# Two-layer graph attention in fp32: mask as a PSUM seed for half of the score banks, and reciprocals on ScalarE and GpSimd

## The chip, the cores and the metric

The kernel runs on one core of a Trainium2 chip. The metric is the device time of one execution in microseconds (us); the median of three runs is used. All data are fp32.

## The reference, cut to what matters

Two layers act on x of shape (64, 256, 512), 64 batches of 256 nodes with 512 features, with one adjacency matrix `adj` (256 x 256) shared by all batches.

```python
h = relu(layernorm(x))
x = x + (adj @ h) @ W0 + b0                       # layer 0
h = relu(layernorm(x))
q, k, v = h @ Wq + bq, h @ Wk + bk, h @ Wv + bv   # layer 1, 8 heads of 64
s = q @ k.T / 8 + (1 - adj) * -1e9                # per batch and head
x = x + softmax(s) @ v @ Wo + bo
```

`adj` holds fractions, so the mask (1 - adj) * -1e9 is large nearly everywhere. The softmax needs the row's largest mask subtracted before the exponential; the kernel calls that row vector `top`.

## The kernel before, in words

**Tiling.** The batches are taken in 32 groups of two (`GB = 2`, `NG = 32`). Layer 0 runs over all groups, from 20 to some 640 us, and leaves each group's residual and its normalized, transposed hidden rows in DRAM. Layer 1 then runs over all groups. A matrix product by a weight is done by `project` (seven quarter products in place of eight) and, from group 2 on (`FIRST2`), by `project2`, which takes three of the seven apart once more, with PSUM banks for inner sums.

**Layer 0.** For each group the generator `layer0(g)` (tiles w_g) is interleaved with `adjacency(g + 1)` (tiles py_g+1). Both use three banks called a, c and b. Banks a and c of w are seeded: ScalarE copies the bias b0 into them, and the matmuls add to it.

**Layer 1, one half of the heads (`qd`) at a time.** The loop is: `attend(g, 0)`, `score(g, 1)`, queries and keys of group g + 1, `attend(g, 1)`, `score(g + 1, 0)`, values of g + 1, then `post(g)`, the output projection.

- `score` works through four pairs of banks, (c, b) = 00, 01, 10, 11. For each pair TensorE writes transposed scores (L974), then VectorE reads both banks with `scalar_tensor_tensor` (L980): scores times 1/8 plus the mask `maskT`, into the tile `a` in SBUF. GpSimd subtracts `top` (L986), except in a few stages where VectorE does it (L984). ScalarE takes the exponential (L991), GpSimd adds the two key halves (L998).
- `attend` forms the denominators `pden` (L1007) and the products with v, `pav` in two banks (L1014). ScalarE copies pden to `den` and sums it (L1023). VectorE inverts it in four pieces (L1027), two at once and two later from group 2 on. `divide` multiplies both pav banks by the inverse (L1045), and `note` sums the inverse on ScalarE (L1039). The sums are checked against a bound at the end (L1174, L1175); where they exceed it, a general path, not taken here, would compute everything again.

**What sets the order.** The program order on each engine is that of the Python code: instructions are queued as the functions are called. `after(n, fn)` puts work off by n ticks of a clock that advances between products. Each engine runs its queue in order, and waits are put in where data require them. DMAs are issued on SyncE, but for the first few on ScalarE.

**PSUM banks.** There are eight, handed out by `bank` (L248) from the list `free_banks` and returned to its end by `give` (L258). A list `whole` keeps, for each bank, whether its last tenant's matmuls wrote all of it. [...] a seeded request needs a bank that is whole. `project2` gives its inner banks back as not whole. Before, an unseeded request takes the first bank in the list:

```python
i = next(i for i in free_banks if seed is None or whole[i])
```

A new tenant's first write to a bank must wait until the last reading of the old tenant has ended.

Of the kernel before, what the change touches and what calls it, by code (L numbers as in the profile page):

```python
# [10 lines left out]
AF = mybir.ActivationFunctionType  # L11
ALU = mybir.AluOpType
AX = mybir.AxisListType
P = 128
EPS = 1e-5
SCALE = 1.0 / 8.0
MASKED = -1000000000.0

BOUND = 1.0e22


def load_weight(nc, pool, w, name):
# [176 lines left out]
def kernel(  # L199
# [16 lines left out]
    nc = tc.nc  # L216
    B, N, D = x.shape
    H, HD = 8, D // 8
    DC = D // P
    NT = N // P  # L220
    GB = 2
    T = GB * NT
    GN = GB * N
    NG = B // GB
    HQ = 2
    HF = D // 2
    assert (N, D, HD, GN) == (256, 512, 64, 512)

    keep = ctx.enter_context(tc.tile_pool(name="keep", bufs=1))
    stats = keep.tile([P, 2, NG * HQ], F32, name="stats")  # L230
    flag = keep.tile([1, 1], I32, name="flag")
# [13 lines left out]

    free_banks, bank_of, whole = list(range(8)), {}, [False] * 8

    def bank(shape, name, seed=None):  # L248

        i = next(i for i in free_banks if seed is None or whole[i])  # L250
        free_banks.remove(i)
        t = psum.tile(shape, F32, tag=f"bank{i}", name=name)
        bank_of[id(t)] = (i, t)
        if seed is not None:
            nc.scalar.copy(t, seed[:, None, :].to_broadcast(shape))
        return t

    def give(t, all_written=True):  # L258
        i = bank_of.pop(id(t))[0]
        free_banks.append(i)  # L260
        whole[i] = all_written
# [16 lines left out]
    X, H0, Q, K, V, OT = {}, {}, {}, {}, {}, {}  # L278
# [229 lines left out]
    FIRST2 = 2  # L508
# [32 lines left out]
    def project2(n, halves, blocks, by_token, name, place, first, done=None, seeds=(), add_up=False):  # L541
# [3 lines left out]
        s = W[n]  # L545
# [66 lines left out]
        yield  # L612
        inner = []
        for a, i, k, own in (("a12", 0, 0, None), ("a22", 1, 0, pc), ("s4", 0, 1, pa)):
            inner.append(Inner(a, i, k, own, bank([P, 2, P], f"{name}{i}{k}")))
            inner[-1].u1()
        p2, p4, p3 = inner
        for p in inner:
            if p is not p3 or add_up:
                p.add(p.sum, 0, 0)  # L620
            else:
                p3.begin(p3.sum, 0, 0)
        p2.own = pb = bank([P, 2, N], f"{name}b")
        p2.only((0, 0), (0, 1), (1, 0), fresh=True)

        for m, n in ((0, N), (1, P)) if add_up else ((slice(0, 3), P),):
            o, u = (t if add_up else t.rearrange("p m (h j) -> p (m h) j", j=P) for t in (p2.o, pb))
# [44 lines left out]
        nc.vector.tensor_tensor(row[:, HF:], row[:, HF:], row[:, :HF], op=ALU.subtract)  # L672

    def seeded(row, name):
        return tuple(bank([P, 2, N], f"{name}{b}", seed=row[:, h * HF:(h + 1) * HF]) for h, b in enumerate("ac"))


    def ready(g, moments_at, scales_at, relus_at, batches=1):
# [280 lines left out]
        else:  # L959
            yield from project2("o", halves, O2.pop(g), True, f"o_{g}", place, add_to, done, seeds, add_up=True)  # L960

    A, AS = {}, {}

    def score(g, qd, sum_delay, exps=(3, 4, 5, 8)):


        pair = [act.tile([P, GB, 2 * NT, N], F32, tag="h", name=f"a_{g}_{qd}_{c}", bufs=2) for c in range(2)]
        for c in range(2):
            for b in range(GB):
                ps = [bank([P, NT * N], f"sc_{g}_{qd}_{c}{b}_{j}") for j in range(2)]  # L970
                q, k = Q[g][qd, b], K[g][qd, b]
                for kt in range(NT):
                    for j in range(2):
                        nc.tensor.matmul(ps[j][:, kt * N:(kt + 1) * N],  # L974
                                         k[j * HD:(j + 1) * HD, c, kt * P:(kt + 1) * P],
                                         q[j * HD:(j + 1) * HD, c, :], start=(kt == 0), stop=True,
                                         skip_group_check=True)
                a = A[c, b] = pair[c][:, b]
                for j in range(2):
                    nc.vector.scalar_tensor_tensor(a[:, j * NT:(j + 1) * NT, :].rearrange("p k n -> p (k n)"),  # L980
                                                   ps[j], SCALE, maskT_f, op0=ALU.mult, op1=ALU.add)
                    give(ps[j])
                if (g == NG - 1 or (g, qd) == (0, 0)) and c + b == 2:
                    after(2, lambda a: nc.vector.tensor_tensor(a, a, top_b, op=ALU.subtract), a)  # L984
                else:
                    nc.gpsimd.tensor_tensor(a, a, top_b, op=ALU.subtract)  # L986
                after(exps[2 * c + b], exponent, a)
                after(sum_delay + 2 * c + b, key_sum, g, qd, c, b)

# [10 lines left out]
    def attend(g, qd):  # L1000


        pd = bank([P, GN], f"pden_{g}_{qd}")
        po = [bank([P, GN], f"pav_{g}_{qd}_{f}") for f in range(2)]
        for b in range(GB):
            for h in range(4):
                nc.tensor.matmul(pd[h * 32:(h + 1) * 32, b * N:(b + 1) * N], ones[:, 0:32], AS[h // 2, b][:, h % 2, :],  # L1007
                                 start=(b == 0), stop=True, tile_position=(0, h * 32), skip_group_check=True)
        for b in range(GB):
            v = V[g][qd, b]  # L1010
            for k in range(NT):
                for f in range(2):
                    for h in range(4):
                        nc.tensor.matmul(po[f][h * 32:(h + 1) * 32, b * N:(b + 1) * N],  # L1014
                                         v[:, k, h * HD + f * 32:h * HD + f * 32 + 32],
                                         A[h // 2, b][:, (h % 2) * NT + k, :],
                                         start=(b + k == 0), stop=(k == NT - 1), tile_position=(0, h * 32),
                                         skip_group_check=True)
        i = g * HQ + qd
        if i == 0:  # L1020
            AS["rest"] = act.tile([P, 4, GN], F32, tag="yT1", name="rest")
        den, rden = AS["rest"][:, 0, :], AS["rest"][:, 1, :]
        nc.scalar.activation(den, pd, AF.Identity, accum_out=stats[:, 0, i:i + 1])  # L1023
        give(pd)

        def invert(c):
            nc.vector.reciprocal(rden[:, c * P:(c + 1) * P], den[:, c * P:(c + 1) * P])  # L1027

        early = 2 if g >= FIRST2 and (g, qd) != (NG - 1, 1) else 4
        for c in range(early):  # L1030
            invert(c)
        if qd == 0:

            last = g == NG - 1
            OT[g] = (xpool if last else act).tile([P, DC, GN], F32, tag="x" if last else "r", name=f"oT_{g}")
            HO[g] = Halves(f"o_{g}", [OT[g][:, :, k * N:(k + 1) * N] for k in range(GB)], 0 if last else 1)

        def note():
            nc.scalar.activation(den, rden, AF.Identity, accum_out=stats[:, 1, i:i + 1])  # L1039

        def divide():
            for c in range(early, 4):
                invert(c)
            for f in range(2):
                nc.vector.tensor_tensor(OT[g][:, 2 * qd + f, :], po[f], rden, op=ALU.mult)  # L1045
                give(po[f])
            after(2 if (g, qd) == (NG - 1, 1) else 3, note)
            wait = 0
            if qd == 0:
                HO[g].sums(nc.gpsimd, ("t1",))  # L1050
            elif g < NG - 2:
                HO[g].sums(nc.gpsimd, ("t3", "t2", "t4"))
            elif g == NG - 2:
                wait = 8
                after(7, HO[g].sums, nc.gpsimd, ("t3",))
                after(8, HO[g].sums, nc.vector, ("t2",))
                after(8, HO[g].sums, nc.gpsimd, ("t4",))
# [77 lines left out]
    run(values(0))  # L1135
    for g in range(NG):
        attend(g, 0)
        load_residual(g)
        if g + 2 < NG:
# [3 lines left out]
        if g == 0:  # L1143
            for n, tag in ((4 * DC, "w0_sb"), (4, "w0_s1"), (4, "w0_s2"), (4, "w0_s4"), (4, "adjT"), (4, "b0_r")):
                t = const.tile([P, n, P], F32, tag=tag, name=f"spare_{tag}")
# [6 lines left out]
        else:  # L1152
            last = post(g - 1, seed_outputs(g - 1))
            run(last, 6)
        attend(g, 1)
        if g + 1 < NG:
            score(g + 1, 0, 5)
# [13 lines left out]

    bad = tmp.tile([P, 2 * NG * HQ], F32, tag="u", name="bad")
    worst = small.tile([P, 1], F32, tag="worst", name="worst", bufs=1)
    nc.vector.tensor_scalar(bad, stats.rearrange("p s i -> p (s i)"), BOUND, None, op0=ALU.is_gt)  # L1174
    nc.vector.tensor_reduce(worst, bad, AX.X, ALU.max)  # L1175
    run(last, 3)
    pf = bank([1, 1], "pf")
    nc.tensor.matmul(pf, worst, ones[:, 0:1], start=True, stop=True)
# [37 lines left out]
```

## Time and profile before

| what | us |
|---|---|
| three timed runs | 2660.87, 2661.75, 2664.04 |
| median | 2661.75 |
| profiled execution, from its first to its last instruction | 2658.7 |

The profiled execution is given as its span alone; the median of the timed runs is 3.05 us above it, which is what lies around the instructions.

| engine | busy us | share |
|---|---|---|
| TensorE, matmuls | 2624.0 | 99% |
| TensorE, weight loads | 2282.2 | 86% |
| GpSimd | 1981.1 | 75% |
| VectorE | 1869.5 | 70% |
| ScalarE | 970.5 | 37% |

Operations that the change touches, with their count, mean duration and the engine:

| line, operation | engine | count | mean ns |
|---|---|---|---|
| L986, top subtracted | GpSimd | 253 | 2369 |
| L980, scores read with the mask | VectorE | 512 | 680 |
| L1027, reciprocal of 128 columns | VectorE | 256 | 919 |
| L1023, denominators to SBUF | ScalarE | 64 | 597 |
| L974, score matmuls (passes) | TensorE | 2048 | 383 |

In the views PE is TensorE's matmul row and PEld its weight loads, DVE is VectorE, ACT ScalarE, POOL GpSimd and SP SyncE. A row of the view in order of time gives the start, the time from the start of the first to the end of the last of several equal instructions, engine, line, operation, and tiles as out<-in with the number of instructions; in brackets stands how long the engine was idle before it and what ended that. A row of the waits gives who waited, for whom, how long in all, how many times, and the longest. An fp32 matmul appears as two passes.

### The profile page before, as it was taken

The numbers are of one execution on the slowest core, as the hardware profiler recorded it, in microseconds if no ns is written. First come the engines' busy times: TensorE is split into PE (matmuls) and PEld (weight loads), VectorE is DVE, ScalarE is ACT, GpSimd is POOL, SyncE is SP. The second block draws the span as 40 slices with busy tenths as digits, with TensorE's granted clock in tenths as the row PEclk, the third lists the DMA queues.
The fourth block names the chain that finished last, engine by engine and source line by source line (L and its number), as shares of the span: only waits on it lengthen the run. The fifth ranks groups of instructions, "written<-read, shape, count | busy, mean of one in ns | idle before, by whom it ended". The sixth has DMA issues, their size and how long they took to land. (4 is left out here: it accounts for less than half of the span.)

```text
span 2658.7 us, 51781 instructions
## 1 busy us (share of the span) xinstructions
PE 2624.0 (99%) x20076; PEld 2282.2 (86%) x20076; DVE 1869.5 (70%) x3864; ACT 970.5 (37%) x1875; POOL 1981.1 (75%) x1838
## 2 busy tenths in 40 slices
PE   7999999999999999999999999999999999999997
PEld 6999899998888888888888888888888888888886
DVE  5878888885467676667677676667677676666677
ACT  3445454443333333333333333333333333333332
POOL 5888888775788777777777777777777777777775
PEclk9999999999999999999999999999999999999999
DMA  5777666665122111111111111111222111111110
GB/s 132 199 193 187 172 166 175 175 158 127 34 60 51 49 49 48 49 49 49 49 48 49 49 49 49 49 48 51 62 66 62 50 49 48 49 49 49 49 48 34
DMA packets 281066, 211.04 MB, mean 79 GB/s; under 512 B 145904, under 2 KB 212976, under 8 KB 280816
## 3 DMA queue, kind: packets, MB, share of 16 engines
q1 hardware_dynamic: 280352, 207.15, 29.9%
q8 instruction: 161, 2.64, 0.4%
q14 instruction: 89, 0.73, 0.1%
q10 hardware_dynamic: 464, 0.52, 0.1%
HBM read 106.96 MB, written 100.66 MB: 78 GB/s over the span
## 5 line engine op out<-in xcount | busy, mean ns | idle before, releaser
L986 POOL TENSOR_TENSOR a<-a,top 128x1024 f32<-128x1024 f32 x253 | 591.2, 2369 | 478.0 <-DVE a L980 478.0
L980 DVE SCALAR_TENSOR_TENSOR a<-sc,maskT 128x512 f32<-128x512 f32 x512 | 311.8, 680 | 122.8 <-PE sc L974 122.8
L998 POOL TENSOR_TENSOR as<-a 128x512 f32<-128x512 f32 x256 | 318.5, 1276 | 3.0 <-ACT a L991 3.0
L991 ACT ACTIVATE a<-a 128x1024 f32<-128x1024 f32 x256 | 270.9, 1058 | 4.3 <-DVE a L984 2.3
L1027 DVE RECIPROCAL rest<-rest 128x128 f32<-128x128 f32 x256 | 224.3, 919 | 36.1 <-ACT rest L1023 36.1
L974 PE MATMUL sc<-q,k 64*128 64x256 f32 x2048 | 239.0, 383 | 0.0
L1014 PE MATMUL pav<-a,v 128*32 128x256 f32 x4096 | 233.6, 379 | 0.0
L974 PEld LDWEIGHTS sc<-q,k 64*128 64x128 f32 x2048 | 194.7, 187 | 44.9 <-issue 26.3
L1014 PEld LDWEIGHTS pav<-a,v 128*32 128x32 f32 x4096 | 133.4, 110 | 87.9
L1023 ACT ACTIVATE rest<-pden 128x512 f32<-128x512 f32 x64 | 38.2, 597 | 417.7 <-PE pden L1007 417.7
L665 DVE TENSOR_TENSOR k<-k,k 128x128 f32<-128x128 f32 (+1 forms) x300 | 96.0, 352 | 126.3 <-PE k L564 123.9
L42 DVE BATCH_NORM_STATS2 st<-x 128x6 f32<-128x512 f32 x256 | 173.1, 676 | 9.4 <-DMA x<-in_x_dram 7.2
L693 ACT ACTIVATE h<-x,nb,rs 128x512 f32<-128x512 f32 x128 | 93.9, 803 | 69.3 <-POOL nb L54 69.2
L820 ACT ACTIVATE h<-x,nb,rs 128x512 f32<-128x512 f32 x128 | 97.2, 808 | 52.2 <-POOL nb L54 49.0
L665 DVE TENSOR_TENSOR x<-o,x 128x128 f32<-128x128 f32 (+1 forms) x360 | 110.9, 349 | 3.4 <-PE o_24b L564 0.3
L665 DVE TENSOR_TENSOR q<-q,q 128x128 f32<-128x128 f32 (+1 forms) x300 | 96.0, 352 | 14.0 <-PE q L564 11.7
L665 DVE TENSOR_TENSOR v<-v,v 128x128 f32<-128x128 f32 (+1 forms) x300 | 95.3, 351 | 14.4 <-PE v L564 11.3
L754 POOL TENSOR_TENSOR hs<-h 128x512 f32<-128x512 f32 x31 | 39.4, 1270 | 73.8 <-ACT h L693 63.7
L446 POOL TENSOR_TENSOR t_o<-oT,t_o 128x512 f32<-128x512 f32 x62 | 79.2, 1277 | 12.3 <-DVE t_o L446 10.0
L446 POOL TENSOR_TENSOR t_y<-yT 128x512 f32<-128x512 f32 (+1 forms) x65 | 81.8, 1258 | 5.9 <-ACT yT L804 5.9
L446 POOL TENSOR_TENSOR t_h<-h1T,t_h 128x512 f32<-128x512 f32 x64 | 82.0, 1282 | 5.0
L52 POOL TENSOR_TENSOR rs<-rs,mhalf 128x2 f32<-128x2 f32 (+1 forms) x97 | 79.5, 820 | 8.1
(4808 smaller groups left out, 6981.8 us busy)
## 6 DMA issues: line engine op xcount, KB each, us to landing
x<-in_x_dram SPq DMA_DIRECT2D x256, 128.0 KB, 3.1
residual<-x SPq DMA_DIRECT2D x256, 128.0 KB, 2.5
hidden<-r SPq DMA_DIRECT2D x128, 256.0 KB, 4.4
h1T<-hidden SPq DMA_DIRECT2D x64, 512.0 KB, 9.7
x<-residual SPq DMA_DIRECT2D x32, 1024.0 KB, 7.7
out_dram<-x SPq DMA_DIRECT2D x62, 512.0 KB, 4.3
w_sb<-in_L_gnn_weight_dram SPq DMA_DIRECT2D x1, 1024.0 KB, 9.8
wq_sb<-in_L_gnn_Wq_dram SPq DMA_DIRECT2D x1, 1024.0 KB, 8.2
```

Source lines behind the costliest of these rows:

```text
L42: nc.vector.bn_stats(st, src)
L446: eng.tensor_tensor(self.t[n][:, c, :], self.operand(p, c), self.operand(q, c), op=ALU.subtract)
L665: nc.vector.tensor_tensor(o, ps, u, op=ALU.add)
L693: nc.scalar.activation(H0[g][:, t, :], xt[:, t, :], AF.Relu, bias=nb[:, t % n:t % n + 1], scale=rs[:, t % n:t % n + 1])
L820: nc.scalar.activation(h1[:, k * NT + t, :], xt[:, k * NT + t, :], AF.Relu, bias=nb[:, t:t + 1], scale=rs[:, t:t + 1])
L974: nc.tensor.matmul(ps[j][:, kt * N:(kt + 1) * N], k[j * HD:(j + 1) * HD, c, kt * P:(kt + 1) * P], q[j * HD:(j + 1) * HD, c, :], start=(kt ...
L980: nc.vector.scalar_tensor_tensor(a[:, j * NT:(j + 1) * NT, :].rearrange("p k n -> p (k n)"), ps[j], SCALE, maskT_f, op0=ALU.mult, op1=ALU.add)
L986: nc.gpsimd.tensor_tensor(a, a, top_b, op=ALU.subtract)
L991: nc.scalar.activation(a, a, AF.Exp)
L998: nc.gpsimd.tensor_tensor(AS[c, b], a4[:, :, 0, :], a4[:, :, 1, :], op=ALU.add)
L1014: nc.tensor.matmul(po[f][h * 32:(h + 1) * 32, b * N:(b + 1) * N], v[:, k, h * HD + f * 32:h * HD + f * 32 + 32], A[h // 2, b][:, (h % 2) * ...
L1027: nc.vector.reciprocal(rden[:, c * P:(c + 1) * P], den[:, c * P:(c + 1) * P])
```

## The change

- **Scores.** At the start of `score` four banks, for the pairs (0, 0) and (0, 1), are seeded by ScalarE with 8 times `maskT`. Their matmuls add to it, and VectorE's reading subtracts `top` in the same instruction. The pairs with c = 1 stay as they were, with the mask added where VectorE reads and `top` subtracted by GpSimd or VectorE.
- **Reciprocals.** But for the very last stage, `den` is inverted by ScalarE as exp(-ln(den)), and GpSimd improves the result by one Newton step of three instructions. The exponential also sums the inverse, so `note` is left to the last stage. These instructions are queued behind the next stage's four seeds (`behind_seeds`).
- **Banks.** `bank` gets an argument `partial`. A request takes the first free bank whose `whole` is true, or false with `partial=True`, and the first free one if there is none of the wanted sort. `project2`'s inner banks, pden and one of the two pav banks ask for `partial=True`; all other requests, in both layers, do not.
- **Order of the attention products.** The loop over the two pav banks is moved outside.
- **Seeds** are made with `mul` in place of `copy`. ScalarE's table set, one with logarithm and exponential, is loaded at the start of the program. The check at the end is turned round (largest of "too large" becomes one minus the smallest of "small enough", one instruction more) and has a lower bound.

```diff
+    nc.scalar.preload_act_table_set("natural_log_exp_and_others")
...
-    def bank(shape, name, seed=None):
-
-        i = next(i for i in free_banks if seed is None or whole[i])
+    def bank(shape, name, seed=None, times=1.0, partial=False):
+
+        i = next((i for i in free_banks if whole[i] != partial), None if seed is not None else free_banks[0])
...
-            nc.scalar.copy(t, seed[:, None, :].to_broadcast(shape))
+            nc.scalar.mul(t, seed, times)
...
-            inner.append(Inner(a, i, k, own, bank([P, 2, P], f"{name}{i}{k}")))
+            inner.append(Inner(a, i, k, own, bank([P, 2, P], f"{name}{i}{k}", partial=True)))
...
-        p2.own = pb = bank([P, 2, N], f"{name}b")
+        p2.own = pb = bank([P, 2, N], f"{name}b", partial=True)
...
+        def banks(c, b, **how):
+            return [bank([P, NT * N], f"sc_{g}_{qd}_{c}{b}_{j}", **how) for j in range(2)]
+
+        masked = {cb: banks(*cb, seed=maskT_f, times=1.0 / SCALE) for cb in ((0, 0), (0, 1))}
+        while behind_seeds:
+            behind_seeds.pop(0)()
         for c in range(2):
             for b in range(GB):
-                ps = [bank([P, NT * N], f"sc_{g}_{qd}_{c}{b}_{j}") for j in range(2)]
+                seen = (c, b) in masked
+                ps = masked[c, b] if seen else banks(c, b)
...
-                                         q[j * HD:(j + 1) * HD, c, :], start=(kt == 0), stop=True,
+                                         q[j * HD:(j + 1) * HD, c, :], start=(kt == 0 and not seen), stop=True,
...
+                    if seen:
+                        nc.vector.scalar_tensor_tensor(o, ps[j].rearrange("p (k n) -> p k n", k=NT), SCALE,
+                                                       top_b[:, 0:NT, :], op0=ALU.mult, op1=ALU.subtract)
+                    else:
+                        nc.vector.scalar_tensor_tensor(o.rearrange("p k n -> p (k n)"), ps[j], SCALE, maskT_f,
+                                                       op0=ALU.mult, op1=ALU.add)
                     give(ps[j])
-                if (g == NG - 1 or (g, qd) == (0, 0)) and c + b == 2:
-                    after(2, lambda a: nc.vector.tensor_tensor(a, a, top_b, op=ALU.subtract), a)
-                else:
-                    nc.gpsimd.tensor_tensor(a, a, top_b, op=ALU.subtract)
+                if not seen:
+                    if (g == NG - 1 or (g, qd) == (0, 0)) and b == 1:
+                        after(2, lambda a: nc.vector.tensor_tensor(a, a, top_b, op=ALU.subtract), a)
+                    else:
+                        nc.gpsimd.tensor_tensor(a, a, top_b, op=ALU.subtract)
...
-        pd = bank([P, GN], f"pden_{g}_{qd}")
-        po = [bank([P, GN], f"pav_{g}_{qd}_{f}") for f in range(2)]
+        pd = bank([P, GN], f"pden_{g}_{qd}", partial=True)
+        po = [bank([P, GN], f"pav_{g}_{qd}_{f}", partial=f == 1) for f in range(2)]
...
-        def invert(c):
-            nc.vector.reciprocal(rden[:, c * P:(c + 1) * P], den[:, c * P:(c + 1) * P])
-
-        early = 2 if g >= FIRST2 and (g, qd) != (NG - 1, 1) else 4
-        for c in range(early):
-            invert(c)
+        final = (g, qd) == (NG - 1, 1)
+
+        def invert():
+
+            nc.scalar.activation(rden, den, AF.Ln)
+            nc.scalar.activation(rden, rden, AF.Exp, scale=-1.0, accum_out=stats[:, 1, i:i + 1])
+            nc.gpsimd.tensor_tensor(den, den, rden, op=ALU.mult)
+            nc.gpsimd.tensor_scalar(den, den, -1.0, 2.0, op0=ALU.mult, op1=ALU.add)
+            nc.gpsimd.tensor_tensor(rden, rden, den, op=ALU.mult)
+
+        if final:
+            for c in range(4):
+                nc.vector.reciprocal(rden[:, c * P:(c + 1) * P], den[:, c * P:(c + 1) * P])
+        else:
+            behind_seeds.append(invert)
...
         def divide():
-            for c in range(early, 4):
-                invert(c)
...
-            after(2 if (g, qd) == (NG - 1, 1) else 3, note)
+            if final:
+                after(2, note)
```

More of the change, by code (lines that the diff above doesn't have):

```diff
@@ L17 @@
 MASKED = -1000000000.0
-BOUND = 1.0e22
+BOUND = 1.0e15
 def load_weight(nc, pool, w, name):
@@ L674, in seeded @@
     def seeded(row, name):
-        return tuple(bank([P, 2, N], f"{name}{b}", seed=row[:, h * HF:(h + 1) * HF]) for h, b in enumerate("ac"))
+        return tuple(bank([P, 2, N], f"{name}{b}", seed=row[:, None, h * HF:(h + 1) * HF].to_broadcast([P, 2, N])) for h, b in enumerate("ac"))
     def ready(g, moments_at, scales_at, relus_at, batches=1):
@@ L960, in post @@
             yield from project2("o", halves, O2.pop(g), True, f"o_{g}", place, add_to, done, seeds, add_up=True)
-    A, AS = {}, {}
+    A, AS, behind_seeds = {}, {}, []
     def score(g, qd, sum_delay, exps=(3, 4, 5, 8)):
         pair = [act.tile([P, GB, 2 * NT, N], F32, tag="h", name=f"a_{g}_{qd}_{c}", bufs=2) for c in range(2)]
+        def banks(c, b, **how):
[3 more added lines that the diff above has]
+            behind_seeds.pop(0)()
         for c in range(2):
             for b in range(GB):
-                ps = [bank([P, NT * N], f"sc_{g}_{qd}_{c}{b}_{j}") for j in range(2)]
+                seen = (c, b) in masked
+                ps = masked[c, b] if seen else banks(c, b)
                 q, k = Q[g][qd, b], K[g][qd, b]
@@ L979, in score @@
                 for j in range(2):
-                    nc.vector.scalar_tensor_tensor(a[:, j * NT:(j + 1) * NT, :].rearrange("p k n -> p (k n)"),
-                                                   ps[j], SCALE, maskT_f, op0=ALU.mult, op1=ALU.add)
-                    give(ps[j])
-                if (g == NG - 1 or (g, qd) == (0, 0)) and c + b == 2:
-                    after(2, lambda a: nc.vector.tensor_tensor(a, a, top_b, op=ALU.subtract), a)
-                else:
-                    nc.gpsimd.tensor_tensor(a, a, top_b, op=ALU.subtract)
+                    o = a[:, j * NT:(j + 1) * NT, :]
+                    if seen:
[4 more added lines that the diff above has]
+                                                       op0=ALU.mult, op1=ALU.add)
+                    give(ps[j])
+                if not seen:
[3 more added lines that the diff above has]
+                        nc.gpsimd.tensor_tensor(a, a, top_b, op=ALU.subtract)
                 after(exps[2 * c + b], exponent, a)
@@ L1008, in attend @@
                                  start=(b == 0), stop=True, tile_position=(0, h * 32), skip_group_check=True)
[L1009 to L1012, printed above, removed]
+        for f in range(2):
+            for b in range(GB):
+                v = V[g][qd, b]
+                for k in range(NT):
                     for h in range(4):
@@ L1173 @@
     worst = small.tile([P, 1], F32, tag="worst", name="worst", bufs=1)
-    nc.vector.tensor_scalar(bad, stats.rearrange("p s i -> p (s i)"), BOUND, None, op0=ALU.is_gt)
-    nc.vector.tensor_reduce(worst, bad, AX.X, ALU.max)
+    nc.vector.tensor_scalar(bad, stats.rearrange("p s i -> p (s i)"), BOUND, None, op0=ALU.is_le)
+    nc.vector.tensor_reduce(worst, bad, AX.X, ALU.min)
+    nc.vector.tensor_scalar(worst, worst, -1.0, 1.0, op0=ALU.mult, op1=ALU.add)
     run(last, 3)
```

## The prediction

> **What bounds the kernel now.** I read the busy shares first, then TensorE's own waits, then one score stage and one layer-0 group in order of time. Busy shares of the page:
>
> ```profile
> PE 2624.0 (99%) x20076; PEld 2282.2 (86%) x20076; DVE 1869.5 (70%) x3864; ACT 970.5 (37%) x1875; POOL 1981.1 (75%) x1838
> ```
>
> TensorE has work for 2624.0 of 2658.7 us. A busy matmul row alone proves little, since ends are modelled; the weight loads at 86% and TensorE's list of waits say the same. Its four longest:
>
> ```profile
> PE pa L331 <- DVE adj_p L326: 10.0, 1, 10.0
> PE o_30a L453 <- DVE x L665: 4.0, 1, 4.0
> PE pden L1007 <- POOL as L998: 2.9, 3, 1.3
> PE py_1a L770 <- ACT yT L789: 2.5, 1, 2.5
> ```
>
> All its waits sum to some 28 us, and none lies between 660 and 2600 us, where PE is busy 1940.00 of 1940. So a VectorE or GpSimd instruction taken away there is worth nothing by itself, and any wait put in front of a matmul is paid in full. (The chain of waits is one DVE row here and tells nothing.)
>
> Two score stages in order of time (start, duration). The usual one, group 15:
>
> ```profile
> 1579.31 3.72 PE L974 MATMUL sc<-q,k 64*128 64x256 f32 x32
> 1582.96 1.16 PEld L453 LDWEIGHTS v_15a<-wv_sb,h1T 128*128 128x128 f32 x6 [0.33 <-issue]
> ```
>
> and VectorE's eight readings of that stage's banks, with the reciprocals and the division behind them:
>
> ```profile
> 1580.55 4.87 DVE L980 SCALAR_TENSOR_TENSOR a<-sc,maskT 128x512 f32<-128x512 f32 x8 [2.01 <-PE sc L974]
> 1585.34 1.75 DVE L1027 RECIPROCAL rest<-rest 128x128 f32<-128x128 f32 x2
> 1587.12 1.29 DVE L1045 TENSOR_TENSOR oT<-pav,rest 128x512 f32<-128x512 f32 x2
> ```
>
> TensorE writes the eight banks in 3.65 us. VectorE starts 1.24 us after TensorE, reads one in 0.68 us and starts one each 0.598 us ((4.87 - 0.68) / 7). It is slower than TensorE here: the stage keeps pace only because TensorE reuses a bank late, its 7th and 8th waiting for readings 1 and 2. The exception shows the price of being caught up, in group 19, where VectorE started late:
>
> ```profile
> 1862.78 4.06 PE L974 MATMUL sc<-q,k 64*128 64x256 f32 x32
> 1866.77 1.56 PE L453 MATMUL q_20a<-h1T,wq_sb 128*128 128x256 f32 x6
> 1864.37 3.08 DVE L980 SCALAR_TENSOR_TENSOR a<-sc,maskT 128x512 f32<-128x512 f32 x5 [2.36 <-PE sc L974]
> ```
>
> The stage takes 3.99 us. In the single rows the 8th bank's first matmul starts at 1865.710, 0.055 after reading 2 ended at 1865.655, and 0.228 later than unhindered; 0.33 are lost, so restarting costs 0.10 more (weights not loaded ahead). The view of waits doesn't list this: the other row half was still busy.
>
> **What the Trainium skill says.** "Perfetto Trace Analysis", Optimizing Tensor Performance, asks that independent matmul groups rotate through different PSUM banks so that evacuation overlaps the next group. Group 15 agrees; the change shortens that rotation. "PSUM — Partial Sum Buffer", The four PSUM rules: a matmul without the start flag adds where an earlier matmul set the bit and overwrites where it didn't. That is what the list `whole` keeps; no row shows the bits. "VectorE: DVE Perf Modes", Why PSUM operands drop a tier: fp32 from PSUM goes at 1x at most. The 0.598 us for 512 columns agrees, and replacing maskT by top leaves it as it is. "ScalarE: Activation LUTs", Table sets: ln and exp share one set, hence one load; before has one load of 1.28 us.
>
> **The change part by part.**
>
> *Instructions moved off.* VectorE loses 252 of 256 reciprocals: 252 x 0.88 (half of 1.75) = 222 us. GpSimd loses 128 of 253 subtractions of 2.37 us, 303 us, and gains 63 chains of two multiplications (1.28 each) and a one-input operation. No row shows that at 128x512; it lies between 0.23 (128x4) and 1.28 (two inputs). "GPSIMD Engine Reference", 3.1's 1.03 cycles an element gives an estimate of 0.44 plus overhead; I take 0.7, so 63 x 3.3 = 205 us. ScalarE gains 256 seeds at 0.52 each (the pitch of the L255 copies), 133 us, and 63 logarithms of 0.60; the exponential replaces `note` (0.63 + 0.19). All of it hides behind TensorE: nothing here shortens 660 to 2600. The cover of the new division: it can start about 1491.7 in group 14 (GpSimd free at 1488.4, plus 3.3), where before it started at 1492.64. At twice the GpSimd price it still ends before v or q need VectorE. No instruction of TensorE is added; the new order of the attention products is the same 64 passes. The table load ahead of ScalarE's DMAs delays adj_r by 1.3 us; it is read at 9.55, its issue ended at 2.6: nothing.
>
> *Seeds.* TensorE now waits for four ScalarE copies. In group 14 ScalarE ends the denominators (L1023, at 1481.57 for 0.60, and its accumulator read) at 1482.25, and four seeds at 0.52 put the two pairs at 1483.3 and 1484.4. The score matmuls want them at 1484.82 and 1485.8. Cover 1.4 us, cost nothing; logarithm and exponential stand behind. In the first stage no attention product covers them: keys end at 642.6, ScalarE evicts them 642.74 to 643.58, two seeds end near 644.6, TensorE wanted to start at 642.63: +2.0 us once.
>
> *Banks in the score stage.* The rewritten `bank` gives an unseeded request the first bank that is `whole`, before older banks that aren't. I followed the list of free banks through the program. From group 2 on, when c=1 asks for its four, the free list holds two banks that aren't whole, left by project2, ahead of those just released: they are passed over, and c=1 gets the four seeded banks. This holds in 60 of 64 stages. The order of the built program confirms it: both pairs of c=1 wait for VectorE. The 8th bank now needs reading 4, not 2. In group 15's times, counted from TensorE's start: reading 4 ends at 1.24 + 3 x 0.598 + 0.68 = 3.71; plus 0.055 gives 3.77; the matmul was due at 2.70; plus the restart of 0.10, TensorE leaves the stage 1.17 us late. 60 x 1.17 = 70 us. The next projection's bank (reading 5, 4.31) is free by then. Two stages of group 0 wait for reading 3 only: 2 x 0.57 = 1.1; the two of group 1 as before.
>
> *Banks in layer 0.* The same preference leaves banks 0, 6 and 7 (not whole) unused and turns five. Then py_b of the next group takes the bank of w_b, which VectorE reads late:
>
> ```profile
> 239.91 0.66 DVE L665 TENSOR_TENSOR x<-w_11b,x 128x512 f32<-128x512 f32 x1
> 240.55 0.97 PEld L770 LDWEIGHTS py_12b<-adjT,h 128*128 128x128 f32 x8
> 240.66 1.06 PE L770 MATMUL py_12b<-adjT,h 128*128 128x128 f32 x8
> ```
>
> The reading ends as TensorE's use begins: 0.1 us with latency, in 20 groups (0 to 0.25 each), 2 us. Where mask or bias steps delay VectorE, I compared the same two times: group 14 1.3, groups 23 to 25 0.45 each, 26 1.0, and twice (py_22c, py_27c) 3.7. Sum 13 us.
>
> *The tail.* The 4.0 us wait at 2620.59 follows from VectorE's readings, t_o sums, two reciprocals (1.75) and the division. Without the reciprocals it ends about 1.3 earlier, and absorbs the last stage's 1.17: 2.5 us back. The other waits there move along.
>
> **Sum.** 70 + 1 + 2 + 13 - 2.5 = 83.5 us on a span of 2658.7. The median of the runs, 2661.75, is 3 us above that span, so I add to the median: 2745.
>
> **Rivals.**
> - *The stall is smaller.* If a late restart overlaps the projection that follows, or the two row halves drift, half of the 1.17 may be left: 35 + 13 = 48 us, 2710. Against it: group 19 lost all.
> - *Seeds late.* If ScalarE holds the first pair about 1.5 us longer than I read, each stage pays that too: at 1 us a stage 64 more, 2810. For: ScalarE is in order. Against: it waits for pden in all 64 places (417.7 us in sum).
> - *Faster.* The wait vanishes if VectorE reads a seeded bank so fast that reading 4 ends by 2.65: 1.24 + 4 d + 0.08 gives d = 0.33 us, the point where it decides, against 0.598. Then only gains stay, the tail's 2.5 and at most the 4.5 of the pden, t_o and rest waits, with the layer-0 stalls absent if its readings speed up too: 2655.
> - *Little moves*, about 2660: bank choice as traced, but its waits covered by something I don't see.
>
> **Chances.** Forecast with its own bounds, 78%: stage 1.0 to 1.35 us, so 60 to 81; layer 0 8 to 20; rest -2 to 4; 2728 to 2767. Smaller stall 9%, late seeds 8%, faster 2%, little 3%. The range 2715 to 2775 takes in the upper part of the smaller stall and a fraction of late seeds. This kernel can be told from no change at about 0.2%. Faster 0.02, same 0.03, slower 0.95.
>
> **What would show it.** The score stage in the profile after should take 4.8 us where it took 3.65, with one reading still each 0.6 us and VectorE's reading 4 ending 0.05 before a matmul; py_22c should wait over 3 us for DVE; banks' seeds should end over 1 us before the scores; PE busy share should drop by some 2 to 3 points if the gaps show as idle. A score stage of 3.7 us makes it wrong; so does a stage that opens with a wait for ACT.

## The result and the profile after

The kernel after takes 2747.51 us in the median of four runs (2745.3 to 2748.0). The kernel before took 2661.32 in the same four rounds, so the ratio is 1.0322, interval 1.0307 to 1.0337: slower by 86 us. The forecast was 2745, its range 2715 to 2775. The profiled execution took 2748.0 us with a span of 2746.2, 87.5 more than before.

Busy shares of the page after:

```profile
PE 2703.2 (98%) x20076; PEld 2302.0 (84%) x20076; DVE 1650.0 (60%) x3613; ACT 1145.4 (42%) x2194; POOL 1885.5 (69%) x1899
```

VectorE does some 220 us less and GpSimd 96 less, ScalarE 175 more: the work has moved as intended. TensorE runs the same 20,076 passes, yet its busy time is 79 us longer, so most of the wait hides in the busy time. The mean pass of the score line has grown from 383 to 401 ns. A score pass is recorded at 0.376 us or more, while on average one starts each 0.114 (32 in 3.65), so the records of earlier passes cover a short wait.

From the list of TensorE's own waits, kernel after (the first two rows here are new and belong to layer 0, the third to the first score stage, the last to the tail):

```profile
...
PE py_22c L771 <- DVE x L666: 3.5, 1, 3.5
PE py_27c L771 <- DVE x L666: 3.5, 1, 3.5
...
PE sc L983 <- ACT sc L256: 1.4, 1, 1.4
...
PE o_30a L454 <- DVE x L666: 1.0, 1, 1.0
```

The large loss isn't in this list. It stands in the weight loads' row of the view of all waits:

```profile
PEld sc L983 <- DVE a L991: 62.2, 182, 0.8
```

VectorE's readings (L991) hold up the weight loads of the scores 182 times, some three times in each of 60 stages. The score stage of group 15 in order of time, kernel after, shows where; the rows are start, duration, engine, line and tiles, as before:

```profile
1626.44 2.15 ACT L256 ACTIVATE sc<-maskT 128x512 f32<-128x512 f32 x4
...
1629.17 4.93 PE L983 MATMUL sc<-q,k 64*128 64x256 f32 x32
...
1630.44 2.48 DVE L991 SCALAR_TENSOR_TENSOR a<-sc,top 128x512 f32<-128x512 f32 x4 [4.27 <-PE sc L983]
1631.18 0.29 PEld L983 LDWEIGHTS sc<-q,k 64*128 64x128 f32 x2 [0.41 <-DVE a L991]
...
1631.78 0.89 PEld L983 LDWEIGHTS sc<-q,k 64*128 64x128 f32 x8 [0.30 <-DVE a L991]
...
1632.84 2.47 DVE L994 SCALAR_TENSOR_TENSOR a<-sc,maskT 128x512 f32<-128x512 f32 x4
1632.97 0.73 PEld L983 LDWEIGHTS sc<-q,k 64*128 64x128 f32 x6 [0.30 <-DVE a L991]
...
1634.03 1.99 PE L454 MATMUL v_15a<-wv_sb,h1T 128*128 128x256 f32 x8
```

The stage goes from 1629.17 to the next projection at 1634.03: 4.86 us, where before it took 3.65. VectorE starts 1.26 after TensorE (before 1.24) and still starts one reading each 0.598. In the single rows the four readings of the seeded banks end at 1631.128, 1631.726, 1632.323 and 1632.920, and TensorE's passes into the c=1 banks start at 1631.182, 1631.781, 1632.378 and 1632.975: 0.055 later each time. From the fifth bank on TensorE follows VectorE, bank for bank. It takes each bank back at once; before, it took back only two, as the 7th and 8th, and found them free. The first of these waits shows how little of it is seen as idle time: the last passes into the seeded banks start at 1630.796 but are recorded until 1631.172, so the row is idle for 0.01 before the pass at 1631.182.

The length is 4.86 in 58 of 64 stages. The sum over all stages is 308.3 us, before 234.7: the difference of 73.6 is most of the result. Where the remainder arises, found by setting the same matmul of the two traces side by side:

| stretch | after minus before, us | forecast |
|---|---|---|
| layer 0, up to the queries of group 0 | 15.5 | 13 |
| first score stage, seeds and gap | 2.4 | 2 (seeds) + 0.57 (bank) |
| all later score stages, up to the tail | 72.6 | 70, and 0.57 for the second stage |
| tail | -3.3 | -2.5 |
| sum, up to the last matmul | 87.3 | 83.5 |

### The profile page after: what moved, and what is told of

It reads as the page before. It is cut to its first block, busy times and chain, and to the rows that moved or that the text cites. A ratio compares the mean times of both kernels' runs of the same rounds, so it can differ in the third digit from the quotient of the medians.

```text
span 2746.2 us, 52052 instructions
## 1 busy us (share of the span) xinstructions
PE 2703.2 (98%) x20076; PEld 2302.0 (84%) x20076; DVE 1650.0 (60%) x3613; ACT 1145.4 (42%) x2194; POOL 1885.5 (69%) x1899
## 5 line engine op out<-in xcount | busy, mean ns | idle before, releaser
L1047 POOL TENSOR_TENSOR rest<-rest 128x512 f32<-128x512 f32 x63 | 80.0, 1270 | 473.5 <-ACT rest L1046 473.5
L1001 POOL TENSOR_TENSOR a<-a,top 128x1024 f32<-128x1024 f32 x125 | 292.4, 2361 | 71.1 <-DVE a L994 71.1
L991 DVE SCALAR_TENSOR_TENSOR a<-sc,top 128x512 f32<-128x512 f32 x256 | 159.0, 683 | 276.6 <-PE sc L983 276.5
L983 PE MATMUL sc<-q,k 64*128 64x256 f32 x2048 | 311.5, 401 | 2.5 <-ACT sc L256 1.4
L983 PEld LDWEIGHTS sc<-q,k 64*128 64x128 f32 x2048 | 209.1, 186 | 105.5 <-DVE a L991 62.2
L994 DVE SCALAR_TENSOR_TENSOR a<-sc,maskT 128x512 f32<-128x512 f32 x256 | 158.2, 679 | 0.0
L256 ACT ACTIVATE sc<-maskT 128x512 f32<-128x512 f32 x256 | 137.5, 591 | 0.0
```

The costliest lines, as they stand in the source:

```text
L256: nc.scalar.mul(t, seed, times)
L983: nc.tensor.matmul(ps[j][:, kt * N:(kt + 1) * N], k[j * HD:(j + 1) * HD, c, kt * P:(kt + 1) * P], q[j * HD:(j + 1) * HD, c, :], start=(kt ...
L991: nc.vector.scalar_tensor_tensor(o, ps[j].rearrange("p (k n) -> p k n", k=NT), SCALE, top_b[:, 0:NT, :], op0=ALU.mult, op1=ALU.subtract)
L994: nc.vector.scalar_tensor_tensor(o.rearrange("p k n -> p (k n)"), ps[j], SCALE, maskT_f, op0=ALU.mult, op1=ALU.add)
```

## The experiments

Each kernel was timed beside the kernel before in the same rounds. A ratio is to that kernel, with its 95% interval.

### The bank rule taken apart: scores, layer 0, both

Three kernels keep everything of the change but the preference for whole banks. In the first, only the unseeded score requests take the oldest free bank again:

```diff
-        i = next((i for i in free_banks if whole[i] != partial), None if seed is not None else free_banks[0])
+        i = next((i for i in free_banks if oldest or whole[i] != partial), None if seed is not None else free_banks[0])
...
-                ps = masked[c, b] if seen else banks(c, b)
+                ps = masked[c, b] if seen else banks(c, b, oldest=True)
```

> The changed kernel, but the two unseeded pairs of each score stage take the oldest free banks again, whole or not. Bank theory: the eighth bank waits for VectorE's reading 2 and no longer for reading 4, so a score stage falls from 4.86 to 3.65 us and the time by 59 x 1.2 = 71 us and another 1 in the first stages: 2675 us. Seed theory (adding onto ScalarE's copies, or waiting for them, is what costs): seeds are as before, stage stays 4.86, 2747 us. Reciprocal theory (ScalarE and GpSimd came onto the path): 2747 us.

Measured 2675.15 us (ratio 1.0059, 1.0044 to 1.0075). Score stage of group 15, this kernel:

```profile
1594.85 3.74 PE L983 MATMUL sc<-q,k 64*128 64x256 f32 x32
...
1598.52 1.99 PE L454 MATMUL v_15a<-wv_sb,h1T 128*128 128x256 f32 x8
```

It takes 3.67 us again, with the seeds and the new readings in place.

In the second kernel only layer 0 has the old rule; `layer[0]` becomes 1 where layer 1 begins:

```diff
-        i = next((i for i in free_banks if whole[i] != partial), None if seed is not None else free_banks[0])
+        i = next((i for i in free_banks if layer[0] == 0 and seed is None or whole[i] != partial), None if seed is not None else free_banks[0])
```

> The changed kernel with the oldest free bank for unseeded requests in layer 0 only. Bank theory: the waits of py_22c, py_27c, py_14b, py_23b to py_26b for VectorE go, and the slow matmuls behind the long ones: start of layer 1 falls by 14 us, stages stay at 4.86: 2733 us. Other theories: 2747 us.

Measured 2731.59 us (1.027, 1.0254 to 1.0285). The score stages take 4.86, and py_22c and py_27c have left the list of waits.

The third has both edits.

> The changed kernel with both: oldest free bank in layer 0 and for the unseeded pairs of the score stages. Seeds and new reciprocals stay. Bank theory: all that is left of the change is +2.3 us at the first score stage, where seeds wait for the keys' eviction, and -3 to -4 us in the tail: 2661 us, within 0.15% of the kernel before. Seed theory: a good part of the 86 us stays, over 2690. Reciprocal theory: the same, over 2690.

Measured 2660.71 us in 13 runs (1.0001, 0.9993 to 1.001). So the whole loss is the rule, and the seeds and the new reciprocals, all still there, gain nothing that shows. The four kernels make a square: the rule in the scores costs 70.9 us with the old layer 0 and 72.4 with the new; the rule in layer 0 costs 14.4 and 15.9. (The second figure of each pair uses the kernel after, timed in other rounds, in which the kernel before took 1.1 us more.)

### The bank rule alone

The kernel before with only the new rule and its `partial=True` requests (for the inner banks, pden and one pav bank, as in the change); no score seeds, no new reciprocals:

```diff
...
+    def bank(shape, name, seed=None, partial=False):
...
+        i = next((i for i in free_banks if whole[i] != partial), None if seed is not None else free_banks[0])
```

> The kernel before with the new rule for banks alone (whole first, the partial requests as in the change): no seeds for scores, no logarithm, reciprocals on VectorE, old order of attention products. Bank theory: score stages of 4.86 us from group 2 on, py_22c and py_27c wait 3.5 us for VectorE; 71 + 14 us slower, without the 2.3 of the first seeds and without most of the 3 that the tail gave back: 2661 + 86 = 2747 us. Seed theory and reciprocal theory: 2661 us.

Measured 2746.03 us (1.0326, 1.031 to 1.0341). The rule alone costs as much as the whole change did. Score stage of group 15, this kernel:

```profile
1622.94 4.90 PE L974 MATMUL sc<-q,k 64*128 64x256 f32 x32
1624.17 4.88 DVE L980 SCALAR_TENSOR_TENSOR a<-sc,maskT 128x512 f32<-128x512 f32 x8 [2.01 <-PE sc L974]
1624.92 0.29 PEld L974 LDWEIGHTS sc<-q,k 64*128 64x128 f32 x2 [0.38 <-DVE a L980]
...
1627.77 1.99 PE L453 MATMUL v_15a<-wv_sb,h1T 128*128 128x256 f32 x8
```

4.83 us from start to start, with the old reading instruction; the forecast's 3.65 + 1.17 is 4.82. The seeds have no part in the stall.

### The reading's pace

If the end of reading 4 sets the end of the stage, slower readings of the seeded banks must lengthen it by the same amount. Here the kernel after reads each seeded bank in four pieces of 128 columns:

```diff
-                        nc.vector.scalar_tensor_tensor(o, ps[j].rearrange("p (k n) -> p k n", k=NT), SCALE,
-                                                       top_b[:, 0:NT, :], op0=ALU.mult, op1=ALU.subtract)
+                        for k in range(NT):
+                            for m in range(2):
+                                nc.vector.scalar_tensor_tensor(o[:, k, m * P:(m + 1) * P],
+                                                               ps[j][:, k * N + m * P:k * N + (m + 1) * P], SCALE,
+                                                               top[:, m * P:(m + 1) * P], op0=ALU.mult, op1=ALU.subtract)
```

> The changed kernel, with each seeded bank read by VectorE in four instructions of 128 columns instead of one of 512. Bank theory: the stage follows the end of reading 4. With about 0.20 us a piece (from rows of 128x128 additions out of PSUM) it ends at 1.24 + 15 x 0.20 + 0.29 = 4.53 us after TensorE's start where it ended at 3.71; the stage grows from 4.86 to 5.68 and the time by 60 x 0.82 = 49 us: 2797 us. If instead a wait of TensorE costs a fixed time, whatever VectorE takes, 2747 us; VectorE is busy 60% of the time and has room for the 256 x 0.2 us.

Measured 2797.69 us (1.0517, 1.05 to 1.0533). Its stage of group 15:

```profile
1651.67 2.00 PE L983 MATMUL sc<-q,k 64*128 64x256 f32 x16
...
1652.94 3.25 DVE L993 SCALAR_TENSOR_TENSOR a<-sc,top 128x128 f32<-128x128 f32 x16 [4.26 <-PE sc L983]
...
1653.97 3.47 PE L983 MATMUL sc<-q,k 64*128 64x256 f32 x16 [0.29 <-DVE a L993]
...
1657.37 0.92 PE L454 MATMUL v_15a<-wv_sb,h1T 128*128 128x256 f32 x3
```

The 16 pieces start each 0.198 us, and the last ends 4.52 after TensorE's start (4.53 forecast). The first 16 passes, into the seeded banks, take 2.00; the second 16 wait for the readings, and the stage takes 5.70. The reader sets the pace, and a cost of the reader is now paid by TensorE.

### The seeds' cover

The kernel with both old rules, each score seed written twice by ScalarE:

```diff
-            nc.scalar.mul(t, seed, times)
+            for _ in range(2 if name.startswith('sc_') else 1):
+                nc.scalar.mul(t, seed, times)
```

> The kernel with the oldest bank in both places (2661 us), and ScalarE writes each score seed twice. Cover as read before the change: 1.4 us behind the second pair; four more copies at 0.52 make the first pair end 0.4 us before it is wanted and the second 0.7 after: 62 x (0.7 + 0.1 for the restart) = 50 us, 2711 us. If seeds don't matter as long as ScalarE has room (43% busy, 144 us more): 2661 us. If they were on the path already: 64 x 2.1 = 134 us, 2795 us.

Measured 2734.28 us (1.0281, 1.0265 to 1.0297): the seeds became the bound, but cost 23 us more than expected. Its stage of group 15:

```profile
1613.93 4.68 ACT L258 ACTIVATE sc<-maskT 128x512 f32<-128x512 f32 x8
1616.66 1.56 PE L985 MATMUL sc<-q,k 64*128 64x256 f32 x10
...
1618.66 2.85 PE L985 MATMUL sc<-q,k 64*128 64x256 f32 x22 [0.44 <-ACT sc L258]
...
1621.45 1.99 PE L456 MATMUL v_15a<-wv_sb,h1T 128*128 128x256 f32 x8
```

Eight seeds take 4.68, more than the 4.23 of 2.15 and 4 x 0.52: the second writing of a bank starts 0.03 after the first has ended, while writings to different banks overlap by 0.07. The last ends at 1618.61, and TensorE goes on at 1618.66. The stage is 4.79 long, 1.12 more than with single seeds. The cover of the change's own seeds can be read in the kernel after: in group 15 the second seed ends 1.62 us before TensorE's first pass into its pair, the fourth 1.55, and in all stages but the first it is the same within 0.02. The forecast had 1.5 and 1.4. So the miss was mainly the price of the edit, not the cover.

Next, logarithm and exponential put ahead of the seeds, which eats 1.41 us of that cover and leaves 0.14:

```diff
-        masked = {cb: banks(*cb, seed=maskT_f, times=1.0 / SCALE) for cb in ((0, 0), (0, 1))}
         while behind_seeds:
             behind_seeds.pop(0)()
+        masked = {cb: banks(*cb, seed=maskT_f, times=1.0 / SCALE) for cb in ((0, 0), (0, 1))}
```

> The same kernel, with logarithm and exponential (1.3 us on ScalarE) ahead of the four seeds instead of behind. Cover theory: 1.4 us of cover hold 1.3: 2661 to 2667 us. If the cover is smaller than I read, up to 62 x 1.3 = 80 us more, 2741 us.

Measured 2660.02 us (1.0004, 0.9995 to 1.0012): no change, stages 3.67. The cover holds from its other side: 1.4 us less of it is free, 2.5 us less is not.

### The first stage without seeds

The kernel with both old rules, and no seeds in the one stage that no attention product covers:

```diff
-        masked = {cb: banks(*cb, seed=maskT_f, times=1.0 / SCALE) for cb in ((0, 0), (0, 1))}
+        masked = {cb: banks(*cb, seed=maskT_f, times=1.0 / SCALE) for cb in ((0, 0), (0, 1)) if g + qd}
```

> The kernel with the oldest bank in both places, and the first score stage without seeds (top subtracted as before there). The wait of that stage for ScalarE goes, and the slow matmuls behind it, 3.8 us in that kernel's trace: 2657 us, 0.14% under both. If the wait is only moved (keys' eviction), 2661 us.

Measured 2657.29 us in 13 runs (0.999, 0.9982 to 0.9998). Beside the kernel with both old rules it gains 3.4 us. In the traces the first stage with its wait is 3.9 shorter, but 1.7 of that is a stretch of half clock which this stage has in the trace of both old rules, and not in that of the kernel with the logarithm first, where the stage's code is the same (see the last section). So some 2.2 us are the seeds' price there; that all of the 3.4 comes from this stage isn't shown. It is the fastest kernel here, ahead of before by 0.1%, less than the 0.2% that a measurement of this kernel tells from no change.

### The reciprocals alone

The kernel before with the new reciprocals, formed as soon as the denominators are in SBUF; no seeds, old rule, so GpSimd keeps all its subtractions of `top`:

```diff
-        for c in range(early):
-            invert(c)
...
+            nc.scalar.activation(rden, den, AF.Ln)
+            nc.scalar.activation(rden, rden, AF.Exp, scale=-1.0, accum_out=stats[:, 1, i:i + 1])
+            nc.gpsimd.tensor_tensor(den, den, rden, op=ALU.mult)
+            nc.gpsimd.tensor_scalar(den, den, -1.0, 2.0, op0=ALU.mult, op1=ALU.add)
+            nc.gpsimd.tensor_tensor(rden, rden, den, op=ALU.mult)
```

> The kernel before with the new reciprocals alone: logarithm and exponential on ScalarE, the Newton step on GpSimd; no seeds, banks and order as before. Theory: hidden everywhere but in the tail, where VectorE is 1.75 us earlier: 2658 to 2661 us. If they were what costs in the change: 2700 or more.

Measured 2681.94 us (1.0082, 1.0068 to 1.0097): 22 us slower where none was expected. The score stages are 3.65; the view of TensorE's waits of this kernel has a new row in nearly every group:

```profile
PE q_4a L454 <- ACT q L908: 0.6, 1, 0.6
```

Group 15 in order of time, this kernel:

```profile
1557.32 1.27 POOL L1034 TENSOR_TENSOR rest<-rest 128x512 f32<-128x512 f32 x1
...
1560.61 9.33 POOL L987 TENSOR_TENSOR a<-a,top 128x1024 f32<-128x1024 f32 x4
...
1563.01 1.06 ACT L992 ACTIVATE a<-a 128x1024 f32<-128x1024 f32 x1 [0.95 <-POOL a L987]
...
1563.97 0.82 ACT L908 ACTIVATE q<-q_15a,bq_c 128x256 f32<-128x256 f32 x2
...
1564.85 1.99 PE L454 MATMUL q_15a<-t_h,wq_s 128*128 128x256 f32 x8 [0.59 <-ACT q L908]
```

GpSimd's three instructions stand ahead of its four subtractions, which start 6.8 us after the scores (1553.81), where before it was 3.6. ScalarE's first exponential (L992) waits for the first subtraction, and the eviction of the queries (L908), whose product ended at 1562.91, stands behind it in ScalarE's queue. That is one reading; another is that the logarithm and exponential themselves delay ScalarE. Moving the Newton step to VectorE was to tell them apart (this cut and the next are against the kernel just shown):

```diff
-            nc.gpsimd.tensor_tensor(den, den, rden, op=ALU.mult)
-            nc.gpsimd.tensor_scalar(den, den, -1.0, 2.0, op0=ALU.mult, op1=ALU.add)
-            nc.gpsimd.tensor_tensor(rden, rden, den, op=ALU.mult)
+            nc.vector.tensor_tensor(den, den, rden, op=ALU.mult)
+            nc.vector.tensor_scalar(den, den, -1.0, 2.0, op0=ALU.mult, op1=ALU.add)
+            nc.vector.tensor_tensor(rden, rden, den, op=ALU.mult)
```

> The kernel with the new reciprocals alone, its Newton step (three instructions) on VectorE in place of GpSimd; logarithm and exponential stay on ScalarE. Theory (GpSimd's chain of 3.2 us stands ahead of the four subtractions of top, so the exponential of the first pair, which waits for the first subtraction, holds up the third eviction of the queries queued behind it on ScalarE): the subtractions start again about 3.6 us after the scores, the wait of q for ACT is gone in all groups, 2661 us, 2658 to 2664. Rival (ScalarE itself is late through the logarithm and the exponential): still 0.85 us in each group, 2682 us.

Measured 2682.09 us (1.0084, 1.0067 to 1.01). By its time the rival had won; by its trace neither had. The wait of q for ScalarE is gone from the list, as the theory said, but 28 of the 64 score stages take some 4.4 us. Group 15, this kernel:

```profile
1554.90 0.75 DVE L1034 TENSOR_TENSOR rest<-rest 128x512 f32<-128x512 f32 x1 [1.66 <-ACT rest L1033]
1555.07 1.72 POOL L538 TENSOR_TENSOR t<-h1T 128x512 f32<-128x512 f32 x1
1555.69 1.38 DVE L1035 TENSOR_SCALAR rest<-rest 128x512 f32<-128x512 f32 x1
1556.08 4.50 PE L975 MATMUL sc<-q,k 64*128 64x256 f32 x32
...
1557.10 1.10 DVE L1036 TENSOR_TENSOR rest<-rest 128x512 f32<-128x512 f32 x1
...
1558.12 4.86 DVE L981 SCALAR_TENSOR_TENSOR a<-sc,maskT 128x512 f32<-128x512 f32 x8
```

The Newton step holds VectorE until 1558.2, so the readings start 2.04 us after the scores, not 1.24, and the stage's 7th and 8th bank are late: the same weak point of the score stage, reached by another way. A kernel with the step left out altogether decides; its inverse is exp(-ln(den)) as ScalarE makes it:

```diff
-            nc.gpsimd.tensor_tensor(den, den, rden, op=ALU.mult)
-            nc.gpsimd.tensor_scalar(den, den, -1.0, 2.0, op0=ALU.mult, op1=ALU.add)
-            nc.gpsimd.tensor_tensor(rden, rden, den, op=ALU.mult)
```

> The kernel with the new reciprocals alone and without the Newton step: the inverse is exp(-ln(den)) as ScalarE makes it, and nothing is added to GpSimd or VectorE. Theory (GpSimd's chain ahead of the subtractions was the whole loss of the reciprocals alone): 2660 us, 2657 to 2663, no wait of q for ACT, score stages 3.65 us. Rival (the logarithm and the exponential on ScalarE delay what stands behind them): about 2682 us, as with the chain on either engine.

Measured 2659.58 us (0.9998, 0.999 to 1.0007), with no wait of q for ScalarE in the list. Logarithm and exponential cost nothing that shows; GpSimd's three instructions ahead of its four subtractions were the whole loss. In the full change the same three instructions are free: the kernel with both old rules has them. There only two subtractions follow them, and the first two exponentials, on seeded pairs, wait for none. In its group 15 the three instructions end at 1557.31, and GpSimd still idles 0.42 us for VectorE's reading before it subtracts at 1557.73. So the reciprocals are free beside the seeds, which make room on GpSimd. Two things this doesn't separate or test: the full change also queues the reciprocals at another place, and no kernel has the seeds without the reciprocals.

## Why the prediction was right, and where it was off

- *The score stage.* The forecast of 1.17 us in each of 60 stages measured 1.20 or 1.21 in 56. All its terms stand: VectorE 1.26 late (1.24), pitch 0.598, release 0.055, one reading the reason. The old rule in the scores takes it away, the rule alone brings it, and slower readings stretch it.
- *"The next projection's bank is free by then".* Held: v_15a starts without a wait for DVE.
- *Group 0 and group 1.* The second stage cost 0.61 (0.57); the stages of group 1 0.09 together, as good as nothing, as said.
- *Layer 0.* 13 forecast, 15.5 measured. The waits were sized well: py_14b 1.2 (1.3), groups 23 to 25 0.38 each (0.45), 26 0.97 (1.0), py_22c and py_27c 3.7 each (3.7); the quiet groups 0.06 or nothing (0.1). What failed is that a wait was taken to end with its release; that the quiet groups cost far less than their 2 us hid a part of it. Kernel after:

```profile
431.03 0.66 DVE L666 TENSOR_TENSOR x<-w_21b,x 128x512 f32<-128x512 f32 x1
...
431.83 2.05 PE L771 MATMUL py_22c<-adjT_t,h 128*128 128x128 f32 x8 [3.54 <-DVE x L666]
...
433.67 2.65 PE L454 MATMUL w_21a<-w_s,t_y 128*128 128x256 f32 x8
...
436.16 1.05 PE L771 MATMUL py_22a<-adjT_t,hs 128*128 128x128 f32 x8
```

  The eight passes after the wait take 2.05 where the same shape takes 1.05 a little later, and the next eight 2.65 in place of 1.89: 1.70 us more for py_22c, 1.51 for py_27c. The view of stretches, kernel after, gives TensorE's granted clock as a share of full speed (PEclk):

```profile
core 0: us, PE busy (x) PEld busy (x) DVE busy (x) ACT busy (x) POOL busy (x), PEclk, DMA share, GB/s
428.39:431.80 3.41, 0.00 (x0) 0.00 (x0) 3.26 (x9) 0.71 (x2) 3.17 (x6) 1.00 0.00 0
431.80:435.21 3.41, 3.38 (x12) 3.14 (x13) 1.10 (x2) 1.29 (x3) 1.66 (x4) 0.50 0.00 0
```

  The clock is 0.50 for just these 3.41 us and 1.00 again behind them; half of 3.41 is the 1.70 lost. The kernel before has such a stretch too (2620.39 to 2623.80): o_30a at 2620.59 takes 3.56 for eight passes after 4.03 us idle. The forecast read the wait there and not the slow passes. Of the rest, 1.8 us belong to the first groups, and they needn't be a cost of the change: in the traces of eight other kernels here with the old rule in layer 0, layer 1 starts between 3.0 us earlier and 0.7 later than in the kernel before, by waits such as that of w_0a.
- *The first stage.* 2.35 in all, for 2.0 of seeds and 0.57 of banks. The seeds took more and the banks less: with the old rule in the scores it still cost 2.17, which leaves 0.2 for the banks.
- *The tail.* -2.5 forecast, -3.3 measured. The wait of o_30a fell from 4.0 to 1.0, and its passes went back from 3.56 to 1.99, by the slow passes overlooked above. Against that, the wait of o_30b for GpSimd, behind it, grew from 0.2 to 1.5, which the forecast didn't have; that the two nearly cancel is luck.
- *Engines.* VectorE lost some 220 (222 from the reciprocals), GpSimd 96 (98), ScalarE gained 175 (some 170). The one-input GpSimd instruction took 0.62 (0.7 estimated; bounds 0.23 and 1.28).
- *"PE busy share should drop by some 2 to 3 points".* It fell by 0.3, from 98.7% to 98.4%. The forecast had itself read in group 19 that such a wait isn't listed, and did not apply this to the busy share.
- *"All of it hides".* True of the whole change, and so of its time; but the forecast did not say on what it rested. It priced the Newton step by GpSimd's sum and by the division that waits for it, and left out what is queued behind it on GpSimd. With all four subtractions behind it, it costs 22 us. That the full change has only two behind it is luck, as far as this forecast goes.
- *The rivals.* Seeds late: the cover was 1.55 us, a little more than read, and 1.41 taken away weren't felt. A smaller stall: no stage from group 2 on took less than 4.86. Faster: the reading's pace stayed at 0.598, far from the 0.33 at which it decides. Little moves: the waits were not covered.

## What to carry to other kernels

An allocator's preference is part of the schedule: which free buffer a request takes says which reading it must wait for, and a reader slower than the writer turns a reuse after six banks into one after four at full price, while the list of waits shows little of it. A wait of TensorE can also cost more than its length: here up to 1.7 us more each time, where the clock went to half behind it. When an instruction is moved to an idle engine, cost what is queued behind it there and who waits for that, not only the engine's sum. A part that is free beside another can cost alone, as the reciprocals do without the seeds, so a part's price is measured with the other both present and absent.

## What the runs showed of the hardware

- After some waits TensorE's granted clock falls to half for 3.41 us. The views of stretches give 0.50 in such a step at py_22c and py_27c (kernel after), at o_30a (kernel before) and in the first score stage of the kernel with both old rules (646.67 to 650.08). That stage took 6.02 us. In the kernel with the logarithm first it took 4.34 at a clock of 1.00, with the same code and after the same wait of 1.42. The wait's length doesn't decide alone: after 2.23 us idle, o_30a met a half-clock step in the traces of three kernels and none in those of three others. In all thirteen traces the clock changes on a grid of 3.41 us. From 20 us on and up to the last matmul, every such step with TensorE's matmul row busy for 0.42 of it or less was followed by a half-clock step. All steps with 0.50 or more were followed by full clock, but one: 1.99 of 3.41 us (0.58) in that first stage with both old rules, while the same 1.99 in the kernel with the logarithm first was followed by full clock. What decides there stays open.
- VectorE and GpSimd slow each other. In the kernel with the Newton step on VectorE, its one-input instruction on 128x512 in SBUF took 0.43 us at all 34 places where GpSimd was idle, and 1.37 or 1.38 at all 29 where GpSimd ran a sum. GpSimd's sum beside it took 1.72 in group 15, where in the kernel with the step on GpSimd the same line took 1.28. The Trainium skill, "SBUF — State Buffer", Who interferes with whom, says that `tensor_scalar` in a two-port mode, and any VectorE instruction with two SBUF inputs against a GpSimd instruction that reads SBUF, contend for a shared pair of ports. The traces agree in kind; that the ports are the reason no run here shows.
- Two ScalarE writings of one PSUM bank in a row did not overlap: eight seeds, two to a bank, took 4.68 us, while four seeds to four banks took 2.15. Whether the engine or a wait in the program keeps them apart isn't shown.
